# A 2x2 group of a filter's Toeplitz blocks by three products in place of four, with the shared product copied into the accumulators

## The chip, the core and the metric

The kernel runs on one core of a Trainium2 chip. The core has five engines, each with an instruction queue of its own: TensorE (matrix products, written to the accumulator memory PSUM), VectorE (elementwise work and reductions), ScalarE (functions of one input, copies), GpSimd (elementwise work, SBUF only in this kernel) and SyncE (it issues the DMA transfers here). In the profile they are PE, DVE, ACT, POOL and SP; PEld is TensorE's weight load. Operands lie in SBUF, 128 partitions wide. All numbers of the kernel are fp32.

The metric is the time of one launch on the device in microseconds, lower is better. Each version is run several times and the median is taken.

## The reference

The reference is one decoder layer on 16 sequences of 256 tokens and 512 channels, in three parts, each with a residual and a layer norm after it: a state-space part (two large projections, a short convolution, a scan), a long convolution along the channels, and a linear layer with eight low-rank experts of which each token takes two. The change is in the second part:

```python
vr = v.reshape(B, H, num_heads, L)       # v: the layer's x; x1 = x2 = ctx
kv = vr[:, :, :, None, :] * x2r[:, :, None, :, :]
y = irfft(rfft(kv, n=2 * L) * rfft(k, n=2 * L)[None, :, None, None, :])[..., :L]
y = y + kv * skip
out = jnp.einsum('bhijl,bhil->bhjl', y, x1r)
```

Here B = 16, L = 512, num_heads = 8 and H = 32. For each of the 32 filters ("heads" below) and each batch, 8 x 8 products `kv` of two signals of length 512 are convolved causally with the filter, multiplied with a third signal and summed over one of the two indices of 8.

## The kernel before

The causal convolution is done as a product with a lower triangular Toeplitz matrix of 512 x 512. It is cut into 4 x 4 blocks of 128: six full blocks below the diagonal and four triangular ones on it. A block depends only on the difference of its block numbers, so blocks (2, 1), (1, 0) and (3, 2) hold the same filter values, and so do (2, 0) and (3, 1). In each triangular block three of four 64 x 64 quadrants are not zero; these 12 quadrants are issued to TensorE's 64 x 64 tiles in three rounds of four (`QUADRANTS`), so that four run side by side. Halves of some blocks are swapped in the order of the channels (`SWAPPED_IN`, `SWAPPED_OUT`), so that each of the four tiles gets three quadrants. The second and the third round are kept apart from the first by a tiny copy on ScalarE, `one`: it waits for the first round, and the third round waits for it.

Stage one (the state-space part) goes over eight groups of 512 tokens and ends near 770 us. Stage two is the loop over `h`, the 32 heads, with software pipelining over neighbouring heads. A head has two halves of the batch, q = 0 and 1. For each half there is one call of `convolve` (six full products and the 12 quadrants, 512 columns wide) into four PSUM tiles of 128 x 512, held as two pairs: `y[0]` and `y[1]`. Each pair has one buffer only. The blocks of a pair in this version are (1, 0) and (3, 2), by `BLOCKS_OUT`; the full blocks come first and the quadrants after them, except where `late` is set (head 0 and the last convolution), where the order is the other way about.

Around a convolution the work is, by its line in the profile:

- VectorE: `products` (L152) makes `kv` of the next head from its turned input `vT` and the context `cT`, two operations for each q. `multiplied` (L963) reads a pair of `y` and makes `pr`; `reduced` (L973) sums it into `red`. L1085 adds this to `o`, which gives the convolution's output `ol`. `skip_sum` (L854) makes `ws`. `gates` (L1007 to L1027) ranks the eight experts by comparisons `cmp`, and ends with `xa`. `finish` (L1040) makes `x3` from the finished linear layer `base`.
- GpSimd: `skip_sums` (L844) makes `sk`; `skip_term` (L861) makes `t`; `with_residual` (L874, L876) makes `o` in three operations; the small steps of the layer norms (L986 to L994, L1045) make `nm`, `var`, `rs` and `nb`.
- ScalarE: copies `vT` (L142) and `xaT` (L1072) out of PSUM, `one` (L951), the sums and squares of the layer norms (L1065, L991), the exponential of the gates (L1011), and the result `res` (L1050).
- TensorE, beside the convolutions: the transposes of `vn` (L140), of `ol` (L1000) and of `xa` (L1070), the gates' logits `gl` (L1115), the linear layer `base` in four blocks (L1120), and its last term `lora` (L1076).
- SyncE: loads of the Toeplitz blocks `T` (L121), of `vn` (L133) and `cT` (L127), and the stores of `out` (L1051).

The order of the work on each engine is the order in which the code is written: the section is under `tc.manual_schedule()`, so nothing is moved by a planner. For head h the code issues: `multiplied` and `reduced` of q = 1 of head h-1; `ol`; `finish` of head h-2; the convolution q = 0; `products` q = 0 of the next head; `multiplied` and `reduced` of q = 0; the transposes and layer norm of `ol` (`centre`), with `skip_term` in between; `gl`; the four blocks of `base`; `gates`; the store; `products` q = 1 of the next head; `skip_sums`; the convolution q = 1, with the transpose of `xa` after its third full block; `lora`; and then the transposes and loads for the head after next. PSUM has eight tiles of 2 KB a partition: two in the pool `ps_t`, two in `ps_s`, four for `y`.

Of the kernel before, what the change touches and what calls it, by code (L numbers as in the profile page):

```python
# [14 lines left out]
P = 128  # L15
# [21 lines left out]
BLOCKS_IN, SWAPPED_IN = (0, 1, 2, 3), (1, 3)  # L37
BLOCKS_OUT, SWAPPED_OUT = (1, 0, 3, 2), (2, 3)

PAIRS = ((2, 0), (3, 0), (3, 1), (2, 1), (1, 0), (3, 2))  # L40
# [3 lines left out]
    (2, 0, 0), (0, 0, 1), (3, 1, 0), (1, 1, 1),  # L44
    (0, 0, 0), (2, 0, 1), (1, 1, 0), (3, 1, 1),
    (3, 0, 0), (1, 0, 1), (2, 1, 0), (0, 1, 1),
)
ER = NE * R
# [17 lines left out]
def decoder_kernel(  # L66
# [44 lines left out]
    ps_s = ctx.enter_context(tc.tile_pool(name="ps_s", bufs=2, space=PSUM))  # L111
# [4 lines left out]
    def load_T(h):  # L116

        both = big.tile([P, NQ * NL * BQ * NH * NH + 10 * P], F32, tag="big", name="kv")
        kv, T = both[:, 0 : NQ * NL * BQ * NH * NH], both[:, NQ * NL * BQ * NH * NH :]
        T = T.rearrange("p (k l) -> p k l", l=P)  # L120
        nc.sync.dma_start(T, toep[h])  # L121
        return kv.rearrange("p (q k b j i) -> p q (k b) j i", q=NQ, k=NL, j=NH, i=NH), T

    def load_c(h):

        cT = q3.tile([P, NQ, 6, BQ * NH], F32, tag="cT", name="cT")
        nc.sync.dma_start(cT, ctxT[h])  # L127
        return cT
# [36 lines left out]
    with ExitStack() as s1:  # L165
# [4 lines left out]
        gp = s1.enter_context(tc.tile_pool(name="gp", bufs=NI))  # L170
        ps_mm = s1.enter_context(tc.tile_pool(name="ps_mm", bufs=4, space=PSUM))
# [328 lines left out]
        for g in range(NG):  # L500
# [307 lines left out]
            if g == 0:  # L808
                skip_bc = wp.tile([P, S], F32, name="skip_bc")
                nc.sync.dma_start(skip_bc, skip.partition_broadcast(P))  # L810
                w_gl = wp.tile([P, KD, NE + ER], F32, name="w_gl")
                nc.sync.dma_start(w_gl, WglT.rearrange("(k p) e -> p k e", p=P))
                w_f = wp.tile([P, KD, D], F32, name="w_f")
                nc.sync.dma_start(w_f, WffnT.rearrange("(k p) o -> p k o", p=P))
                w_lb = wp.tile([ER, D], F32, name="w_lb")
                nc.sync.dma_start(w_lb, loraB)
                b_bc = wp.tile([P, D], F32, name="b_bc")
                nc.sync.dma_start(b_bc, b_ffn.partition_broadcast(P))
                gb_bc = wp.tile([P, NE], F32, name="gb_bc")
                nc.sync.dma_start(gb_bc, gate_b.partition_broadcast(P))  # L820

                tri = wp.tile([P, NE, NE], F32, name="tri")
                nc.gpsimd.memset(tri, 0.0)
                for e in range(1, NE):
                    nc.gpsimd.memset(tri[:, e, 0:e], 1.0)
                share = wp.tile([P, P], F32, name="share")
                nc.gpsimd.memset(share, 1.0 / D)
# [4 lines left out]
    with ExitStack() as s2:  # L832
        p2 = s2.enter_context(tc.tile_pool(name="r2", bufs=2, reuse_waits="tile"))
        ps_y = s2.enter_context(
# [36 lines left out]
        def with_residual(t, vT):  # L871

            o = p2.tile([P, NQ, NL, BQ * NH], F32, tag="o", name="o")
            nc.gpsimd.tensor_tensor(o[:, :, 1:3], t[:, :, 0::3], vT[:, :, 0::3], ALU.add)  # L874
            for a, b in ((0, HP), (HP, 0)):
                nc.gpsimd.tensor_tensor(  # L876
                    o[b : b + HP, :, 0::3],
                    t[a : a + HP, :, 1:3],
                    vT[a : a + HP, :, 1:3],
                    ALU.add,  # L880
                )
            return o
# [24 lines left out]

        def convolve(y, kv, T, q, between=None, pairs=PAIRS, late=False, early=None):

            begun = set()

            def full(lb, mb, stop):
                nc.tensor.matmul(  # L916
                    bank_of(y, lb),
                    T[:, PAIRS.index((lb, mb)), :],
                    moving(kv, q, mb),
                    start=not late and lb not in begun,  # L920
                    stop=stop,
                    skip_group_check=True,
                )
                begun.add(lb)

            def quadrant(lb, r, c):
                rows, cols = slice(r * HP, (r + 1) * HP), slice(c * HP, (c + 1) * HP)
                start = lb not in begun and (lb, c) not in begun
                begun.add((lb, c))
                return nc.tensor.matmul(  # L930
                    bank_of(y, lb)[cols],
                    T[rows, len(PAIRS) + lb, cols],
                    moving(kv, q, lb)[rows],
                    start=start,
                    stop=False,
                    skip_group_check=True,
                )

            def full_blocks():
                for n, (lb, mb) in enumerate(pairs):  # L940
                    if n == 1 and early is not None:
                        early()
                    if n == 3 and between is not None:
                        between()
                    full(lb, mb, n >= len(pairs) - 2)

            if not late:
                full_blocks()
            begin = [quadrant(*e) for e in QUADRANTS[:4]]
            one = p2.tile([P, 1], F32, tag="one", name="one")  # L950
            seen = nc.scalar.copy(one, nhalf[:, 0:1])  # L951
            for ins in begin:
                wait_for(seen, ins)
            for e in QUADRANTS[4:8]:
                quadrant(*e)
            for e in QUADRANTS[8:]:
                wait_for(quadrant(*e), seen)
            if late:
                full_blocks()

        def multiplied(y, cT, q, i):
# [4 lines left out]
                cT[:, q, 4 * i : 4 * i + 2].rearrange("p k (b i) -> p k b i", i=NH)  # L966
# [85 lines left out]

        vT_next, vns = heads["vT"], heads["vn"]
        sk_next = skip_sums(0, kvs[0][0])
        vT_after = turned_v(vns.pop(0))
# [12 lines left out]
        def turned_gates(xa):  # L1068
            xat = ps_s.tile([ER, P], F32, tag="s", name="xat")
# [8 lines left out]
        last, done = None, None  # L1078
        for h in range(HX):
            nxt, ff = h + 1 < HX, last is not None  # L1080
            if ff:
                o_f, red_f, y_f, cT_f = last
                contract(y_f, cT_f, red_f, 1, (0, 1) if h == 1 else (1, 0))
                o_l = p2.tile([P, NL, P], F32, tag="ol", name="ol")
                nc.vector.tensor_tensor(  # L1085
# [6 lines left out]
            (kv, T), cT, vT = kvs.pop(0), cTs.pop(0), vT_next  # L1092
            red = p2.tile([P, NQ, NL, BQ * NH], F32, tag="red", name="red")
            y = new_y()
            convolve(y, kv, T, 0, pairs=FIRST if h == 1 else PAIRS, late=h == 0)
            ws = skip_sum(sk_next)
            behind = None
            if nxt:
                kv_n, cT_n, vT_next = kvs[0][0], cTs[0], vT_after
# [3 lines left out]
            def skip():  # L1103
                skips.append(skip_term(cT, ws, behind))

            contract(y, cT, red, 0, (1, 0) if h else (0, 1))
            if ff:
                rs = centre(o_l, skip)
            else:
                skip()  # L1110
            o = with_residual(skips[0], vT)
            if ff:
                gl = ps_s.tile([P, NE + ER], F32, tag="s", name="gl")
# [4 lines left out]
                base = ps_s.tile([P, D], F32, tag="s", name="base")  # L1118
                for kc in range(KD):
                    nc.tensor.matmul(  # L1120
                        base, o_l[:, kc, :], w_f[:, kc, :], start=(kc == 0), stop=False
                    )
                xa = gates(gl, rs)
            if ready is not None:
                store(*ready)
            if nxt:
                products(vT_next, cT_n, kv_n, 1)
                sk_next = skip_sums(h + 1, kv_n)
            turned = []

            def turn():
                if ff:
                    turned.append(turned_gates(xa))

            y = new_y()
            if nxt:
                convolve(y, kv, T, 1, turn, FIRST if h == 0 else PAIRS, h == 0)
                if ff:
                    lora(base, turned)
            else:  # L1140
                y.append(ps_t.tile([P, BQ * NH * NH], F32, tag="tr", name="y2"))
                convolve(y, kv, T, 1, lambda: lora(base, turned), FIRST, True, turn)
            if ff:
                done = (h - 1, base, rs)
            if h + 2 < HX:
                vT_after = turned_v(vns.pop(0))
                kvs.append(load_T(h + 2))
                if h + 3 < HX:
                    vns.append(load_v(h + 3))
                    cTs.append(load_c(h + 3))  # L1150
# [5 lines left out]
        gl = ps_s.tile([P, NE + ER], F32, tag="s", name="gl")  # L1156
        base = ps_s.tile([P, D], F32, tag="s", name="base")
        o_l = {}

        def contracted(src, ks):  # L1160
# [4 lines left out]
            cs = 0 if ks[0] < 2 else 2  # L1165
# [42 lines left out]
        ready = finish(*done)  # L1208
        contracted(y_f[2].unsqueeze(1), (3,))
# [90 lines left out]
```

## Time and profile before

| | |
|---|---|
| median of three runs | 1501.47 us (1500.52 to 1502.03) |
| the profiled execution | 1501.61 us |
| its span, first to last instruction | 1499.8 us |
| granted TensorE clock in it | 0.998 |
| stage two, first quadrant to the end | 771.1 to 1499.8 us |
| from one head to the next | 22.46 us |
| DMA, share of the queues' time over the span | 0.20 |

A row of the profile's groups gives the line, the engine, the operation, the output and inputs by the program's names, the tile's shape and the count, then the busy time and the mean length of one; then the engine's idle time just before, and what ended it. A row of the timeline gives start and length in us, the engine and line, and a count where neighbours are merged. Idle time of an engine that is not the bottleneck costs nothing. Matmul rows overlap, because products are pipelined, so the spacing of their starts says more than their lengths.

### The profile page before, as it was taken

To read this page: it belongs to the slowest core of one execution; us is meant where nothing else is said; L and a number is where in the kernel's file an instruction comes from. 1 tells how busy PE (TensorE), PEld (TensorE's weight loads), DVE (VectorE), ACT (ScalarE), POOL (GpSimd) and SP (SyncE) were. 2 spreads that over 40 slices of the span, in tenths; PEclk is the share of its full clock that TensorE was granted. 3 is DMA by queue.
4 is the path that set the end of the run, shared out by engine and by line. 5 is a ranking of instruction groups with operands and counts; after the bars stand their busy time and mean duration, and the time that the engine had idled before them with its cause. 6 is when DMAs were issued, how large, how long until landed. Compare 5 with 4: busy or idle time off the path is not lost.

```text
span 1499.8 us, 18739 instructions
## 1 busy us (share of the span) xinstructions
PE 1480.3 (99%) x6952; PEld 936.5 (62%) x6952; DVE 1179.8 (79%) x2124; ACT 372.1 (25%) x843; POOL 367.9 (25%) x536
## 2 busy tenths in 40 slices
PE   9999999999999999999999999999999999999997
PEld 8777788887888878888754444444444444444443
DVE  5978778787787877878667778778778778778776
ACT  2522323233232322323101122122122122122121
POOL 7340010100101002010022243243243243243242
PEclk9999999999999999999999999999999999999999
DMA  8014021121111211112022212212212212212200
GB/s 284 31 36 133 18 69 43 36 79 36 52 43 36 79 43 49 38 37 86 8 95 70 85 49 78 85 50 78 85 49 78 84 50 78 84 50 78 84 33 21
DMA packets 50810, 97.46 MB, mean 65 GB/s; under 512 B 10656, under 2 KB 15008, under 8 KB 50720
## 3 DMA queue, kind: packets, MB, share of 16 engines
q1 hardware_dynamic: 50192, 96.28, 19.8%
q8 instruction: 54, 0.88, 0.2%
q14 instruction: 36, 0.29, 0.1%
q10 hardware_dynamic: 528, 0.00, 0.0%
HBM read 78.95 MB, written 17.32 MB: 64 GB/s over the span
## 4 chain that ended last, share of the span: by engine, by line
PE 92%; DVE 5%; DMA 1%; issue 1%; ACT 0%; POOL 0%; SPq 0%; POOLq 0%; DVEq 0%
PE y L916 22%; PE mm L302 17%; PE y L930 12%; PE s L302 11%; PE base L1120 7%; PE s L702 6%; PE mm L702 5%; PE base L1076 2%; PE gl L1115 2%; DVE acc L533 1%; PE tr L1000 1%; PE mm L788 1%; PE mm L661 1%; PE yps L604 1%; PE xm L543 1%; PE tr L140 1%
## 5 line engine op out<-in xcount | busy, mean ns | idle before, releaser
L916 PE MATMUL y<-kv 128*128 128x512 f32 x768 | 348.4, 597 | 0.3 <-DVE pr L963 0.3
L963 DVE TENSOR_TENSOR pr<-y,cT 128x1024 f32<-128x1024 f32 x126 | 148.5, 1219 | 129.6 <-PE y L930 126.0
L916 PEld LDWEIGHTS y<-kv 128*128 128x128 f32 x768 | 141.4, 191 | 158.9 <-issue 154.8
L930 PE MATMUL y<-kv 64*64 64x512 f32 x1536 | 179.6, 598 | 3.3 <-DVE xt L803 1.7
L152 DVE TENSOR_TENSOR kv<-vT,cT 128x1024 f32<-128x1024 f32 x128 | 150.4, 1217 | 1.4 <-ACT vT L142 1.4
L533 DVE SCALAR_TENSOR_TENSOR acc<-xi,wc,acc 128x512 f32<-128x512 f32 x192 | 145.9, 774 | 5.7
L973 DVE TENSOR_REDUCE red<-pr 128x128 f32<-128x1024 f32 x126 | 147.1, 1209 | 0.0
L930 PEld LDWEIGHTS y<-kv 64*64 64x64 f32 x1536 | 52.2, 132 | 122.3 <-issue 96.5
L1120 PE MATMUL base<-w_f,ol 128*128 128x512 f32 x248 | 111.5, 592 | 0.0
L302 PE MATMUL mm<-XT,w_z 128*128 128x256 f32 x384 | 90.7, 379 | 0.0
L302 PEld LDWEIGHTS mm<-XT,w_z 128*128 128x128 f32 x384 | 73.0, 190 | 9.9
L844 POOL TENSOR_TENSOR sk<-kv,skip_bc 128x512 f32<-128x512 f32 x32 | 47.3, 1480 | 115.1 <-DVE kv L152 115.1
L1120 PEld LDWEIGHTS base<-w_f,ol 128*128 128x128 f32 x248 | 44.8, 190 | 44.5 <-issue 44.5
L350 POOL TENSOR_TENSOR rstd<-ms,nhalf 128x4 f32<-128x4 f32 x8 | 8.1, 1018 | 257.9 <-DVE ms L348 257.9
L302 PE MATMUL mm<-xnT,w_z 128*128 128x256 f32 x288 | 70.0, 379 | 0.0
L986 POOL TENSOR_SCALAR nm_c<-sum_c 128x1 f32<-128x1 f32 x31 | 7.2, 231 | 249.4 <-DVE x L1040 249.4
L61 POOL TENSOR_TENSOR rs_a<-ve_a,nhalf 128x1 f32<-128x1 f32 x32 | 19.0, 594 | 189.0 <-DVE ve_a L59 180.5
L302 PEld LDWEIGHTS mm<-xnT,w_z 128*128 128x128 f32 x288 | 54.7, 190 | 10.9 <-issue 3.8
L302 PE MATMUL s<-XT,w_xi 128*128 128x256 f32 x256 | 60.5, 379 | 0.4 <-DVE XT L206 0.4
L302 PE MATMUL mm<-XT,w_xi 128*128 128x256 f32 x256 | 60.5, 379 | 0.0
L991 ACT ACTIVATE sq<-x,nm_c 128x512 f32<-128x512 f32 x31 | 22.4, 722 | 136.5 <-POOL nm_c L986 132.2
L302 PEld LDWEIGHTS s<-XT,w_xi 128*128 128x128 f32 x256 | 48.6, 190 | 7.3 <-POOL w_xi L216 0.8
(266 smaller groups left out, 2545.6 us busy)
## 6 DMA issues: line engine op xcount, KB each, us to landing
kv<-in_toep SPq DMA_DIRECT2D x32, 640.0 KB
cT<-in_ctxT SPq DMA_DIRECT2D x32, 384.0 KB
xt<-in_x SPq DMA_DIRECT2D x32, 256.0 KB
xnT<-in_xT SPq DMA_DIRECT2D x8, 1024.0 KB
spread<-both SPq DMA_DIRECT2D x32, 256.0 KB
first<-xt SPq DMA_DIRECT2D x32, 256.0 KB
vn<-first SPq DMA_DIRECT2D x32, 256.0 KB
out<-res SPq DMA_DIRECT2D x31, 256.0 KB
```

Source lines behind the costliest of these rows:

```text
L152: last = nc.vector.tensor_tensor(kv[:, q, k * BQ : (k + NL // 2) * BQ], vT[:, q, blks].rearrange("p k (b i) -> p (k b) i", i=NH).unsqueeze ...
L302: nc.tensor.matmul(ps, w[:, p, a, kc, :], Xs[b][:, kc, :], start=start and kc == 0, stop=stop and kc == 1, skip_group_check=upon,)
L533: nc.vector.scalar_tensor_tensor(acc, xi[:, :, k : k + S], wc[:, c, k : k + 1], acc, ALU.mult, ALU.add)
L702: nc.tensor.matmul(ps, own[a][c][:, n * P : (n + 1) * P], w_o[b][c], start=start and c == 0, stop=stop and c == HC - 1, skip_group_check=upon,
L844: nc.gpsimd.tensor_tensor(sk, own, skip_bc[:, h * NH : (h + 1) * NH].unsqueeze(1).to_broadcast(full), ALU.mult,)
L916: nc.tensor.matmul(bank_of(y, lb), T[:, PAIRS.index((lb, mb)), :], moving(kv, q, mb), start=not late and lb not in begun, stop=stop, skip_ ...
L930: return nc.tensor.matmul(bank_of(y, lb)[cols], T[rows, len(PAIRS) + lb, cols], moving(kv, q, lb)[rows], start=start, stop=False, skip_gro ...
L963: nc.vector.tensor_tensor(pr.rearrange("p (k b j) i -> p k b j i", k=2, j=NH), y[i].rearrange("p k (b j i) -> p k b j i", j=NH, i=NH), cT[ ...
L973: nc.vector.tensor_reduce(red[:, q, 2 * i : 2 * i + 2, :].rearrange("p k t -> p (k t)"), pr, AX.X, ALU.add)
L1076: nc.tensor.matmul(base, turned[0], w_lb, start=False, stop=True)
L1115: nc.tensor.matmul(gl, o_l[:, kc, :], w_gl[:, kc, :], start=(kc == 0), stop=(kc == KD - 1))
L1120: nc.tensor.matmul(base, o_l[:, kc, :], w_f[:, kc, :], start=(kc == 0), stop=False)
```

## The change

The 2 x 2 group of outputs 2 and 3 with inputs 0 and 1 has the blocks (2, 0), (2, 1), (3, 0) and (3, 1), of which (2, 0) and (3, 1) are equal. With T2 for these two, the outputs are T2 (x0 + x1) + (T1 - T2) x1 for block 2 and T2 (x0 + x1) + (T3 - T2) x0 for block 3. So three products stand for four:

- `prepared` gives the pair sum `xs` = x0 + x1 for each q and the two differences of blocks `Td`, on GpSimd, during the head before.
- `seeded` issues the shared product to a PSUM tile `yc`; ScalarE copies it into both tiles of `y[1]`, which now holds the blocks 3 and 2. The four remaining full products of a convolution and the quadrants add to `y` after that (`begun` starts with blocks 2 and 3, so no product of theirs starts afresh).
- Head 0's first convolution and the last convolution of all (`late`) keep six products.

The halves are swapped in another choice of blocks, so that equal blocks have equal layout. Of the diagonal, two triangles share one loaded block (`TRIANGLE_AT`); a quadrant of block 2 (`AGAIN`) is computed from a copy of the lower half of its input in the upper 64 partitions, `kvd`, made by two ScalarE copies a head (`again`). `T` has 7 blocks in place of 10, `cT` 7 parts in place of 6.

Around this: the pool `ps_s` lives in stage one only, and stage two gets `ps_b` with one tile for `yc` and one for `base`. `ol` is added on GpSimd, not VectorE. The last of the four blocks of `base`, the transpose of `xa` and `lora` move to the start of the next head, between its `multiplied` and `reduced`; so do the transposes of `vn` and the loads. `gates` comes after `products` of q = 1. The load of `lora_B` moves to the start of stage two. The last head keeps the earlier order of these.

```diff
+GIVEN = ((3, 2), (3, 0), (2, 0), (1, 0), (0, 0), (2, 2), (3, 3))
+FULL_AT = {(3, 2): 0, (2, 1): 0, (3, 0): 1, (2, 0): 2, (3, 1): 2, (1, 0): 3}
+TRIANGLE_AT = (4, 4, 5, 6)
...
 QUADRANTS = (
-    (2, 0, 0), (0, 0, 1), (3, 1, 0), (1, 1, 1),
-    (0, 0, 0), (2, 0, 1), (1, 1, 0), (3, 1, 1),
-    (3, 0, 0), (1, 0, 1), (2, 1, 0), (0, 1, 1),
+    (0, 0, 0), (3, 0, 1), (1, 1, 0), (2, 1, 1),
+    (2, 0, 0), (0, 0, 1), (3, 1, 0), (2, 0, 1),
+    (1, 0, 0), (1, 0, 1), (0, 1, 0), (3, 1, 1),
 )
+AGAIN = (2, 0, 1)
...
+            nc.gpsimd.tensor_tensor(o[:, :, 3], t[:, :, 0], vT[:, :, 0], ALU.add)
             for a, b in ((0, HP), (HP, 0)):
                 nc.gpsimd.tensor_tensor(
-                    o[b : b + HP, :, 0::3],
+                    o[b : b + HP, :, 0:3],
...
+        def prepared(kv, T):
+            xs = p2.tile([P, NQ, BQ * NH * NH], F32, tag="xs", name="xs")
+            Td = p2.tile([P, 2, P], F32, tag="Td", name="Td")
+            def pair_sum(q):
+                return nc.gpsimd.tensor_tensor(
+                    xs[:, q], moving(kv, q, 0), moving(kv, q, 1), ALU.add
+                )
+            def differences():
+                nc.gpsimd.tensor_tensor(
+                    Td, T[:, 0:2], T[:, 2:3].to_broadcast([P, 2, P]), ALU.subtract
+                )
+            return xs, Td, pair_sum, differences
+        def again(kv):
+            kvd = p2.tile([P, NQ, BQ * NH * NH], F32, tag="kvd", name="kvd")
+            for q in range(NQ):
+                nc.scalar.copy(kvd[HP:, q], moving(kv, q, 2)[0:HP])
+            return kvd
+        def seeded(y, T, xs, q):
+            yc = ps_b.tile([P, BQ * NH * NH], F32, tag="yc", name="yc")
+            nc.tensor.matmul(yc, T[:, 2, :], xs[:, q], start=True, stop=True)
+            nc.scalar.copy(y[1], yc.unsqueeze(1).to_broadcast([P, 2, BQ * NH * NH]))
...
+            begun = set() if late else {2, 3}
...
+                if (lb, r, c) == AGAIN:
+                    r, src, at = 1 - r, kvd[:, q], TRIANGLE_AT[3]
...
             if not late:
-                full_blocks()
+                full(1, 0, T[:, FULL_AT[1, 0], :])
+                full(3, 2, T[:, FULL_AT[3, 2], :])
+                full(3, 0, Td[:, 1, :])
+                full(2, 1, Td[:, 0, :])
...
+                order = (1, 0)
+                prs = [multiplied(y_f, cT_f, 1, i) for i in order]
+            y = new_y()
+            if h:
+                if rest is not None:
+                    base, o_r, xa = rest
+                    feed_forward(base, o_r, (3,))
+                    turned = turned_gates(xa)
+                seeded(y, T, xs, 0)
+                if rest is not None:
+                    lora(base, [turned])
+                if nxt:
+                    vT_after = turned_v(vns.pop(0))
+                    kvs.append(load_T(h + 1))
...
+            if ff:
+                for i, pr in zip(order, prs):
+                    reduced(pr, red_f, 1, i)
-                nc.vector.tensor_tensor(
+                nc.gpsimd.tensor_tensor(
                     o_l.rearrange("p k (q t) -> p k q t", q=NQ),
...
             contract(y, cT, red, 0, (1, 0) if h else (0, 1))
+            y = new_y()
+            def meanwhile():
+                skips.append(skip_term(cT, ws, behind))
+                if nxt:
+                    seeded(y, T, xs, 1)
             if ff:
-                rs = centre(o_l, skip)
+                rs = centre(o_l, meanwhile)
...
                 products(vT_next, cT_n, kv_n, 1)
+                more_next = prepared(kv_n, T_n)
+                more_next[2](0)
+                more_next[3]()
                 sk_next = skip_sums(h + 1, kv_n)
+                more_next[2](1)
+            if ff:
+                xa = gates(gl, rs)
             if nxt:
-                convolve(y, kv, T, 1, turn, FIRST if h == 0 else PAIRS, h == 0)
+                convolve(y, kv, T, Td, kvd, 1)
+                kvd_next = again(kv_n)
+                rest = (base, o_l, xa) if ff else None
```

## The prediction

> **What bounds the kernel now.** I read the busy totals first, then the costliest groups, then one head of the second stage in the timeline and in a table of windows, then the waits.
>
> The page's busy shares, and the table of windows for one head (columns: window, length, busy time of TensorE, its weight loads, VectorE, ScalarE, GpSimd, then granted clock, DMA share, GB/s):
>
> ```profile
> PE 1480.3 (99%) x6952; PEld 936.5 (62%) x6952; DVE 1179.8 (79%) x2124; ACT 372.1 (25%) x843; POOL 367.9 (25%) x536
> 1059.04:1081.50 22.46, 22.46 (x102) 9.65 (x100) 18.02 (x27) 4.52 (x12) 8.04 (x12) 1.00 0.22 71
> ```
>
> TensorE works through the whole 22.46 us of a head, VectorE 18.0, ScalarE 4.5, GpSimd 8.0. A busy TensorE row need not be a full one, so I look at how densely it is issued. The timeline of the head (start, length, engine, line, what, count):
>
> ```profile
> 1067.12 0.66 PE L1000 MATMUL tr<-ident,ol 128*128 128x128 f32 x4
> 1067.24 2.36 DVE L963 TENSOR_TENSOR pr<-y,cT 128x1024 f32<-128x1024 f32 x2 [0.54 <-PE y L930]
> ...
> 1067.61 1.09 PE L1115 MATMUL gl<-w_gl,ol 128*128 128x136 f32 x8
> ...
> 1068.54 3.60 PE L1120 MATMUL base<-w_f,ol 128*128 128x512 f32 x8
> ...
> 1071.98 2.74 PE L916 MATMUL y<-kv 128*128 128x512 f32 x6
> ```
>
> Eight base records take 1071.98 - 1068.54 = 3.44 us, 0.43 each. An fp32 product is two records, so a full 128x128x512 product costs 0.86 us. The next row starts where this one ends; nothing stands between. A head is 12 full products in two convolutions, two triangles of 2.74 us (12 quadrants of 64x64, four at a time), four base products, and small ones. The waits agree:
>
> ```profile
> DVE pr L963 <- PE y L930: 126.0, 61, 3.6
> ```
>
> VectorE waits for TensorE some 2 us before each pair of `pr`, while the whole page has only 0.3 us of TensorE idle ahead of full blocks and 3.3 ahead of quadrants. So TensorE's own work sets the 22.46 us.
>
> **What the skill says.** PSUM — Partial Sum Buffer, "The four PSUM rules": writes by ScalarE neither set nor clear the written bits; a matmul that doesn't start a group adds onto such data where an earlier matmul set the bit. The first head's convolutions set them, so the seed is added to; no run here shows a seed yet. The same page on bank collisions: different column tiles may write one bank at once, different row tiles may not. The trace shows the first half:
>
> ```profile
> 261.57 1.07 PE L543 MATMUL xm<-acc,mean 128*32 128x512 f32 x8
> ```
>
> Four column tiles into one bank, 3.44 us if serial, take 1.0. SBUF — State Buffer, "Who interferes with whom": a VectorE instruction with two SBUF inputs and a GpSimd one that reads SBUF block each other. The trace agrees: GpSimd's `rs_c` lasts 1.43 us beside the products of VectorE, and `cmp` on 64 elements 0.75 us until a GpSimd op is over:
>
> ```profile
> 1064.35 2.35 DVE L152 TENSOR_TENSOR kv<-vT,cT 128x1024 f32<-128x1024 f32 x2
> 1065.69 1.43 POOL L994 TENSOR_TENSOR rs_c<-var_c,nhalf 128x1 f32<-128x1 f32 x1
> ...
> 1071.61 1.52 POOL L876 TENSOR_TENSOR o<-t,vT 64x256 f32<-64x256 f32 x2
> 1072.47 0.75 DVE L1018 TENSOR_TENSOR cmp<-cmp,tri 128x64 f32<-128x64 f32 x1
> ```
>
> **The change, part by part.** *Products.* Each of 62 convolutions (all but the first and the last) goes from six full products to four, plus the shared one into `yc`: 62 x 0.86 = 53.3 us less of TensorE, 1.72 a head, hence 20.74. The quadrants stay twelve; the triangle is taken as 2.74.
>
> *Seed.* One ScalarE copy of 128x512 into 128x1024. `vT` (512 columns from PSUM) takes 0.59 us and `xaT` (128) 0.27, so 0.83 ns a column: 1.01 us for 1,024. Bounds: 0.59 (the read alone), and twice the estimate, 2.0, if PSUM to PSUM is slow.
>
> Put zero at the end of the second convolution of a head. TensorE does: last base block 0.86, `xat` 0.14, `yc` 0.86, `lora` 0.96, `vn` transposes 0.44, together 3.26. From there full blocks 3.44 + 0.18, triangle 2.74: end at 9.62. Then transposes 0.49, `yc` 0.86, `gl` 0.93, three base blocks 2.58: 14.48. Then 3.44 + 0.08 + 2.74: 20.74. This is the measured spacing of today's rows in the new order.
>
> Is each input there? `y0` must have been multiplied before the first full block: VectorE starts 0.12 after zero and needs 2.35 for two, done at 2.5, wanted at 3.26. The seed waits for `y1` (1.3) and `yc` (1.86), so about 2.0 to 3.0; the second full block wants it at 4.12. In the other half `y0` is done at 12.1, the seed at 12.0 (behind the statistics' first pass on ScalarE), wanted at 14.48 and 15.34. So the seed costs nothing under the moved base block, `lora`, `gl` and transposes; uncovered it would cost 1.3 + 1.0 + one `yc` 0.86 twice a head. A copy of 2.1 us would begin to show.
>
> *ScalarE* gets two seeds and two `kvd` copies (0.59 each from the same row): 4.5 + 3.2 = 7.7 of 20.74. Behind the seed wait the squares, hence `rs_b`, one us later; behind `kvd` only `xaT`. The `one` copies release the last four quadrants. In the first half `one` follows the square of `x3`, about 7.3, wanted near 8.6. In the second it now follows the exponential of the late gates, about 17.5 or a little more, wanted near 19.7. Both have room.
>
> *GpSimd* gets `ol` (1.08, from the 512-element row `t`), two pair sums (1.08 each) and the differences (256 elements, 0.73 as `o`); `o` is regrouped into 128, 384 and 384 elements, about 0.55 + 0.9 + 0.9 = 2.35 on the line through these two rows, in place of 2.2. 8.0 + 4.2 = 12.2 of 20.74. `ol` is ready near 6.0, wanted at 9.62. The pair sums come before 23 and are wanted from 21.7 and from 30.8; the differences are ready near 20, wanted near 26.
>
> *VectorE* loses `ol` (0.61). First half: 0.12 + 2.27 `pr` + 2.44 `red` + 0.67 `x3` + 0.60 `ws` + 2.35 products = 8.45, under 9.62. Second half, from 9.74: 2.27 + 2.26 + 2.35 + gates 2.56 = 19.2, under 20.86. It may come 2.35 us later before TensorE waits: `xat` wants the gates at 21.6, and `y0` must be done by 24.0.
>
> That margin is what GpSimd may eat. The products now come ahead of the gates and meet the `o` ops (two of about 0.9), and the gates meet pair sum, differences and `sk`. Each two-input VectorE op that meets a GpSimd op waits between nothing and the whole of it. In stage one six such ops took 6.78 us beside 256-element sums (1.13 each against an average 0.76 busy), so half an op is a fair wait:
>
> ```profile
> 60.48 6.78 DVE L533 SCALAR_TENSOR_TENSOR acc<-xi,wc,acc 128x512 f32<-128x512 f32 x6
> ```
>
> Half of two `o` ops, of one pair sum twice and of differences is 2.3; less the 0.53 that `cmp` waits already, I take 1.5 more. Lower end 0; upper end, whole ops: 0.9 + 0.9 + 1.08 + 0.55 + 1.48 = 4.9. At 1.5 nothing reaches TensorE.
>
> *DMA and rest.* Per head T falls 640 to 448 KB and `cT` rises 384 to 448. The loads of T, `vn` and `cT` move past `yc`, `lora` on TensorE, but their wait is the same convolution; T is first read by the differences, some 16 us later. The queue behind holds only `out`, whose `res` comes later. DMA share is 0.22; hidden. `lora_B` is loaded at the start of stage two, wanted two heads later. The first head has no covering work between its convolutions: about 0.2 lost.
>
> Sum: 1499.8 - 53.3 + 0.2 = 1446.7 for the span; this run took 1501.61, so 1.8 lies around it: 1448.5. The median of the runs is 0.1 lower. I say 1449.
>
> **Rivals.**
> 1. *GpSimd holds VectorE up.* For it: the waits above; six two-input ops against a train of GpSimd ops. Against: 2.35 us of room. An extra wait of 2.4 to 3.9 costs 0 to 1.5 a head, over 30 heads up to 45; middle 0.7, so 1449 + 21 = 1470. At the upper end of 4.9 it would be 2.55 a head, 1526; from 4.1 on the gain is gone.
> 2. *The seed copy is the wait.* A copy above 2.1 us, or ScalarE late for another reason, costs its excess once a head: 0.5 gives 1449 + 15 = 1464. Against: 1.1 us of room in the tighter half.
> 3. *Quadrants stop running four at a time* (the other side). Each of the second and third rounds now has two quadrants in one bank, before all four in different ones. In the second round they are also of different row tiles, which the skill warns of and no row shows. One serial pair is 0.86 on 64 convolutions, +55: 1504, no change. If both rounds pay, +110: 1559. It decides from 0.83 us a convolution on. Against: each pair writes different partitions, and `xm` shows column tiles sharing a bank at full rate.
>
> **How the numbers follow.** TensorE stays fed 0.64 (1445 to 1453); rival 1 short of the loss 0.17; rival 2 0.03; so faster 0.84. One serial pair or stalls that just eat the gain 0.04, within 0.2% (3 us, about what a measurement can tell). Slower 0.12: rival 3 in full 0.07, rival 1 beyond 4.1 0.05. The range 1444 to 1486 holds the likeliest case, rival 2 and nearly all of rival 1's gaining part, 0.81; the likeliest alone has 1445 to 1453.
>
> **What would show it.** Right: heads 20.7 us apart, TensorE's rows touching, triangles still 2.74, the seed near 1.0 us and `pr` of VectorE still waiting for quadrants. Rival 1: `xat` or the first full block waiting for VectorE, `cmp`, `ex` or products stretched. Rival 2: full blocks waiting for ScalarE. Rival 3: triangles of 3.6 us or more. Wrong at the root would be a full product not saved: L916's successor with other than 768 - 248 + 124 `y` and `yc` records.

## The result, and the profile after

| | before | after |
|---|---|---|
| median | 1501.03 us (1500.52 to 1502.03, 4 runs) | 1445.14 us (1444.09 to 1447.89, 4 runs) |
| ratio, 95% interval | | 0.963, 0.9613 to 0.9646 |
| profiled execution, its span | 1501.61, 1499.8 | 1447.89, 1446.1 |
| from one head to the next | 22.46 | 20.61 |

The change is faster by 55.9 us; 1449 was forecast, a gain of 52.5 from the 1501.47 known then. The busy totals of the changed kernel, and its table of windows over one head (columns as before):

```profile
PE 1425.9 (99%) x6828; PEld 915.6 (63%) x6828; DVE 1215.7 (84%) x2093; ACT 464.4 (32%) x969; POOL 567.8 (39%) x662
1039.82:1060.43 20.61, 20.61 (x97) 8.93 (x96) 19.11 (x26) 7.46 (x16) 14.41 (x16) 1.00 0.23 71
```

TensorE is as full as before over a head that is 1.85 us shorter. VectorE now has 19.11 of 20.61, before 18.02 of 22.46, although an addition left it. The profiled execution of after is the slowest of its four. Part of that lies ahead of the change: the first transposes of `vn` come at 766.85 us, before at 764.60. Another 1.3 us is one long head, shown below. From the first product of `kv` (768.11 and 765.85) to the end it is 678.0 against 734.0, 56.0 less, which is the difference of the medians to 0.1 us.

The timeline of the same head, after. First the start of the head, where the moved work and the seed stand:

```profile
1036.46 0.35 DVE L1074 SCALAR_TENSOR_TENSOR xa<-gl,den,ex 128x128 f32<-128x128 f32 x1
1036.59 1.12 PE L1133 MATMUL base<-w_f,ol 128*128 128x512 f32 x2
1036.76 2.35 DVE L1010 TENSOR_TENSOR pr<-y,cT 128x1024 f32<-128x1024 f32 x2
...
1037.56 0.27 PE L1123 MATMUL xat<-ident,xa 128*128 128x128 f32 x1
...
1037.67 1.02 PE L947 MATMUL yc<-xs,kv 128*128 128x512 f32 x2
...
1038.77 1.00 ACT L948 COPY y<-yc 128x1024 f32<-128x1024 f32 x1 [0.64 <-PE yc L947]
...
1039.82 1.88 PE L959 MATMUL y<-kv 128*128 128x512 f32 x4
...
1041.54 1.88 PE L959 MATMUL y<-kv,Td 128*128 128x512 f32 x4
...
1043.35 1.51 PE L977 MATMUL y<-kv 64*64 64x512 f32 x11
```

The convolution before ends at 1036.59. The seed lasts 1.00 us and is there at 1039.77, and the second full product, which adds to it, starts 0.86 after 1039.82. The four full products take 1039.82 to 1043.35, 3.53 us. The triangle goes from 1043.35 to 1046.09, 2.74. No product waits in this head. The same two rows before:

```profile
1059.04 5.42 PE L916 MATMUL y<-kv 128*128 128x512 f32 x12
...
1064.38 2.81 PE L930 MATMUL y<-kv 64*64 64x512 f32 x24
```

There the six full products took 1059.04 to 1064.38, 5.34 us, and the triangle, up to the next row at 1067.12, 2.74.

Then what GpSimd and VectorE do to each other, in the second half of the head before that:

```profile
1030.16 3.15 DVE L158 TENSOR_TENSOR kv<-vT,cT 128x1024 f32<-128x1024 f32 x2
1030.25 3.92 POOL L885 TENSOR_TENSOR o<-t,vT 64x384 f32<-64x384 f32 x2
...
1033.56 0.69 DVE L1063 TENSOR_TENSOR cmp<-lg 128x64 f32<-128x64 f32 x1
...
1034.24 1.27 POOL L924 TENSOR_TENSOR xs<-kv 128x512 f32<-128x512 f32 x1
1034.31 1.29 DVE L1065 TENSOR_TENSOR cmp<-cmp,tri 128x64 f32<-128x64 f32 x1
```

The two products take 3.15 us, before 2.35. The first `cmp` waits about 0.5 and the third 1.1 (the second, of the same shape, takes 0.21). As a result `xa` ends at 1036.81, 0.2 us after the convolution, and `pr` follows without a wait. TensorE wants `xa` at 1037.56: 0.75 us are left.

One head of this execution shows the edge. From the end of one head's second convolution to the next the others take 20.6 us (all but the first and the last), this one 21.9:

```profile
1221.66 1.48 POOL L853 TENSOR_TENSOR sk<-kv,skip_bc 128x512 f32<-128x512 f32 x1
1221.90 1.26 DVE L1069 SCALAR_TENSOR_TENSOR ex<-rank,ex 128x8 f32<-128x8 f32 x1 [0.48 <-ACT kvd L939]
...
1223.90 0.30 PE L1123 MATMUL xat<-ident,xa 128*128 128x128 f32 x1 [0.68 <-DVE xa L1074]
```

VectorE starts `ex` half a microsecond later than in other heads. Why is not to be seen. So `sk` has begun on GpSimd first, and `ex` takes 1.26 us in place of 0.19. Now the transpose waits 0.68 us for `xa`, and the first full product comes 0.94 later than in other heads. VectorE is late from there on, and the first triangle of the head takes 3.08 us in place of 2.74; two runs below, with one more operation and with `one` ahead, show by which chain.

### The profile page after: what moved, and what is told of

Same layout as the page of the kernel before. It is cut to its first block, busy times and chain, and to the rows that moved or that the text cites. A ratio compares the mean times of both kernels' runs of the same rounds, so it can differ in the third digit from the quotient of the medians.

```text
span 1446.1 us, 18895 instructions
## 1 busy us (share of the span) xinstructions
PE 1425.9 (99%) x6828; PEld 915.6 (63%) x6828; DVE 1215.7 (84%) x2093; ACT 464.4 (32%) x969; POOL 567.8 (39%) x662
## 4 chain that ended last, share of the span: by engine, by line
PE 90%; DVE 6%; issue 1%; DMA 1%; ACT 1%; POOL 0%; SPq 0%; POOLq 0%; DVEq 0%; ACTq 0%
PE mm L309 18%; PE y L959 15%; PE s L309 12%; PE y L977 12%; PE base L1133 8%; PE s L709 6%; PE mm L709 5%; PE yc L947 4%; PE gl L1198 2%; PE base L1129 2%; DVE acc L540 2%; PE tr L1047 1%; PE mm L795 1%; PE mm L668 1%; PE yps L611 1%
## 5 line engine op out<-in xcount | busy, mean ns | idle before, releaser
L158 DVE TENSOR_TENSOR kv<-vT,cT 128x1024 f32<-128x1024 f32 x128 | 180.0, 1447 | 1.4 <-ACT vT L148 1.4
L959 PE MATMUL y<-kv 128*128 128x512 f32 x272 | 128.1, 594 | 2.1 <-DVE pr L1010 1.2
L885 POOL TENSOR_TENSOR o<-t,vT 64x384 f32<-64x384 f32 x64 | 121.1, 1892 | 4.4
L959 PE MATMUL y<-kv,Td 128*128 128x512 f32 x248 | 116.5, 592 | 0.0
L959 PEld LDWEIGHTS y<-kv,Td 128*128 128x128 f32 x248 | 47.1, 190 | 59.3 <-issue 59.1
L959 PEld LDWEIGHTS y<-kv 128*128 128x128 f32 x272 | 49.0, 190 | 53.9 <-issue 50.6
L924 POOL TENSOR_TENSOR xs<-kv 128x512 f32<-128x512 f32 x63 | 80.4, 1276 | 2.4
L948 ACT COPY y<-yc 128x1024 f32<-128x1024 f32 x62 | 61.8, 997 | 34.0 <-PE yc L947 23.8
L1165 POOL TENSOR_TENSOR ol<-o,red 128x512 f32<-128x512 f32 x31 | 39.5, 1273 | 83.3 <-DVE red L1020 83.3
L977 PE MATMUL y<-kvd,kv 64*64 64x512 f32 x128 | 65.2, 589 | 0.0
```

What stands on the lines that cost most here:

```text
L158: last = nc.vector.tensor_tensor(kv[:, q, k * BQ : (k + NL // 2) * BQ], vT[:, q, blks].rearrange("p k (b i) -> p (k b) i", i=NH).unsqueeze ...
L885: nc.gpsimd.tensor_tensor(o[b : b + HP, :, 0:3], t[a : a + HP, :, 1:4], vT[a : a + HP, :, 1:4], ALU.add,)
L924: return nc.gpsimd.tensor_tensor(xs[:, q], moving(kv, q, 0), moving(kv, q, 1), ALU.add)
L948: nc.scalar.copy(y[1], yc.unsqueeze(1).to_broadcast([P, 2, BQ * NH * NH]))
L959: nc.tensor.matmul(bank_of(y, lb), w, moving(kv, q, mb), start=not late and lb not in begun, stop=False, skip_group_check=True,)
L977: return nc.tensor.matmul(bank_of(y, lb)[cols], T[rows, at, cols], src[rows], start=start, stop=False, skip_group_check=True,)
```

## The experiments

**Six products again.** In the changed kernel, convolutions get six full products and no seed; everything moved stays.

```diff
-            begun = set() if late else {2, 3}
+            begun = set()
-                full(1, 0, T[:, FULL_AT[1, 0], :])
-                full(3, 2, T[:, FULL_AT[3, 2], :])
-                full(3, 0, Td[:, 1, :])
-                full(2, 1, Td[:, 0, :])
+                for lb, mb in ((2, 0), (3, 0), (3, 1), (2, 1), (1, 0), (3, 2)):
+                    full(lb, mb, T[:, FULL_AT[lb, mb], :])
...
-                seeded(y, T, xs, 0)
...
-                    seeded(y, T, xs, 1)
```

> The changed kernel with the six full products of before in every convolution, no shared product and no seed; everything moved stays where the change put it, and the pair sums and differences are still computed, without use. Theory (the gain is TensorE's 62 saved products): 62 x 0.86 = 53.3 us come back, 1498 (1495 to 1502). Rival (the gain comes from the moved work, the addition on GpSimd or the new order): below 1475.

Measured: 1533.53 us, 2.2% slower than the kernel before (ratio 1.0216, 1.0201 to 1.0231). Both expectations fail. 88 us come back, 35 more than the products. Its timeline shows where the 35 are:

```profile
1060.98 3.56 DVE L158 TENSOR_TENSOR kv<-vT,cT 128x1024 f32<-128x1024 f32 x2
...
1066.36 1.56 DVE L1063 TENSOR_TENSOR cmp<-cmp,tri 128x64 f32<-128x64 f32 x1
...
1069.81 0.30 PE L1121 MATMUL xat<-ident,xa 128*128 128x128 f32 x1 [0.39 <-DVE xa L1072]
...
1070.47 1.13 PE L1127 MATMUL base<-w_lb,xaT 128*128 128x512 f32 x2 [0.36 <-ACT xaT L1123]
```

Without the seed on ScalarE the statistics of `ol` come earlier, so GpSimd's two long additions of `o` start 0.44 us ahead of the products, where in the changed kernel they start with them. The meetings fall out worse: products 3.56, the third `cmp` 1.56, and the transpose of `xa` waits. Then `lora` waits for the copy of `xa`. In the changed kernel the shared product covers this copy: it keeps TensorE at work while the copy is made.

**The same without the sums.** The pair sums and differences, unused in the run above, are left out, which takes three operations from GpSimd's work of a head.

> As the run with six full products, but the pair sums and differences, which nothing reads there, are left out too. In that run the gates ended late (five of their operations beside GpSimd) and the transpose of xa waited. Theory (62 products are worth 53 us, the other 35 were VectorE held up by GpSimd): the gates are in time again; without the shared product between xa's transpose and lora up to 0.3 us a head stays: 1498 to 1510. Rival (the moved work costs 35 us by itself whenever the six products are back): 1525 and above.

Measured: 1515.12 us. `xa` is in time, and 18 us are gone, but the time lies between the two expectations. The rest is the second wait, larger than I had put it:

```profile
1062.69 0.27 PE L1119 MATMUL xat<-ident,xa 128*128 128x128 f32 x1
...
1063.32 1.12 PE L1125 MATMUL base<-w_lb,xaT 128*128 128x512 f32 x2 [0.36 <-ACT xaT L1121]
```

From the transpose to `lora` are 0.63 us, of which the transpose is 0.11: 0.52 of waiting a head.

**And with a cover.** In addition, the transposes of `vn` go ahead of `lora`.

```diff
+                if nxt:
+                    vT_after = turned_v(vns.pop(0))
                 if rest is not None:
                     lora(base, [turned])
                 if nxt:
-                    vT_after = turned_v(vns.pop(0))
                     kvs.append(load_T(h + 1))
```

> As the run with six full products and without the sums, but lora comes after the transposes of vn, so that they cover the copy of xa. In that run lora waited 0.52 us a head for this copy. Theory (the saved products alone make the difference to the changed kernel): 31 x 0.44 = 14 us come back, 1515 - 14 = 1501, that is 1445 + 53 + at most 3. Rival (the moved work holds TensorE in another way): 1508 and above.

Measured: 1502.60 us (1501.82 to 1503.32, 12 runs), ratio to before 1.0008 (0.9999 to 1.0016): as long as the kernel before within 0.2%, and 1.6 us above the 1501 of the theory. Its head lasts 22.50 us:

```profile
1049.00:1071.50 22.50, 22.50 (x100) 9.77 (x99) 19.24 (x26) 5.66 (x14) 10.18 (x14) 1.00 0.19 65
```

So the moved work, in this order and without the sums, is neither gain nor loss. The whole gain, 55.9 us against before and 57.5 against this run, is the products and the small gaps that go with them. The first run was 30.9 us slower than this one: 18.4 went with the sums, whose work had made `xa` late, and 12.5 with the wait for the copy of `xa`. The other 4 of its 35 are the small gaps.

**The seed twice.**

```diff
-            nc.scalar.copy(y[1], yc.unsqueeze(1).to_broadcast([P, 2, BQ * NH * NH]))
+            for _ in range(2):
+                nc.scalar.copy(y[1], yc.unsqueeze(1).to_broadcast([P, 2, BQ * NH * NH]))
```

> The changed kernel with the seed copied twice, so 2.0 us in place of 1.0. Theory (the seed is hidden; in the tighter half it was there 0.9 us before the second full product wants it, in the other 3 us): at most 0.1 us a head, 1445 to 1449. Rival (the seed is what the convolution waits for): 1 us a head or two, 1475 or 1505.

Measured: 1454.82 us, 9.7 more than the changed kernel, 0.31 a head for 1.0 us more in each half. In the timeline:

```profile
1060.90 2.02 ACT L949 COPY y<-yc 128x1024 f32<-128x1024 f32 x2 [0.64 <-PE yc L947]
...
1061.95 2.15 PE L960 MATMUL y<-kv 128*128 128x512 f32 x4
...
1063.94 1.88 PE L960 MATMUL y<-kv,Td 128*128 128x512 f32 x4
```

The seed ends at 1062.92 and the second full product was due at 1062.81; with the way from ScalarE to TensorE it starts 0.27 late, and the four-record row is 2.15 long in place of 1.88. In the other half nothing waits. The time is above the 1445 to 1449 of the theory and far below the rival's 1475. So the single seed is hidden, but the room in the tighter half is about 0.7 us, not 0.9: the second product starts 0.16 us after the seed's end, and this way between the engines had been left out.

**One more operation on GpSimd.**

```diff
                 more_next[2](0)
+                more_next[2](0)
                 more_next[3]()
```

> The changed kernel with the first pair sum done twice on GpSimd, one more 128x512 operation of 1.27 us right beside the gates. Theory (VectorE has room left): ex waits about 0.7 us more, the gates end just before the transpose of xa wants them, 0 to 0.2 us a head, 1445 to 1451. Rival (what GpSimd takes from VectorE is already passed on to TensorE): 0.7 us or more a head, 1465 and above.

Measured: 1459.02 us, 13.9 more, 0.46 a head: more than the theory allowed, less than the rival. `xa` behaves as expected, and the transpose comes 0.06 us late; with it the first full product of the head comes 0.15 late. The larger part is elsewhere, in the first half:

```profile
1067.14 1.21 POOL L1033 TENSOR_SCALAR nm_c<-sum_c 128x1 f32<-128x1 f32 x1
...
1068.39 0.72 ACT L1038 ACTIVATE sq<-x,nm_c 128x512 f32<-128x512 f32 x1 [3.80 <-POOL nm_c L1033]
...
1069.11 0.18 ACT L993 COPY one<-nhalf 128x1 f32<-128x1 f32 x1
...
1069.34 1.09 PE L977 MATMUL y<-kv 64*64 64x512 f32 x8
```

`nm_c`, one element a partition, takes 1.21 us beside the products of VectorE. The square of `x3` waits for it, `one` stands behind the square in ScalarE's queue, and the third round of quadrants waits for `one`. The triangle takes 1067.27 to 1070.36, 3.09 us. In the changed kernel `nm_c` takes as long (1042.75 to 1043.96). What is new is that VectorE leaves the gates later, so that `x3` starts 1.94 us after the first full product in place of 1.46, and the chain behind it ends too late.

**The same with `one` ahead.** In the first half the convolution is issued between `nm_c` and the square, so that `one` comes first.

```diff
-            nm, rs = centred_squares(x3, total, "c")
+            nm, rs = centred_squares(x3, total, "c", between)
...
-            ready = finish(*done) if done is not None else None
-            convolve(y, kv, T, Td, kvd, 0, late=h == 0)
+            def first_half():
+                convolve(y, kv, T, Td, kvd, 0, late=h == 0)
+            ready = finish(*done, first_half) if done is not None else first_half()
```

> The run with one more pair sum on GpSimd, but in the first half the copy one is issued to ScalarE ahead of the square of x3. In that run the triangle of the first half took 3.09 us in place of 2.74, since one stood behind the square, the square behind nm, and nm behind the products. Theory (one is the tightest point): 0.35 us a head comes back, 1459 - 10 = 1449 (1446 to 1452). Rival (the late gates alone cost the 14 us): 1457 to 1460.

Measured: 1448.68 us, 10.3 less than with `one` behind. So the chain from `nm_c` to the quadrants is what cost 10.3 of the 13.9. The other 3.5 fit the head's start, where the first full product still comes 0.15 us late.

**`one` ahead, nothing else.**

> The changed kernel with one issued ahead of the square of x3 in the first half, nothing else. Theory (one comes just in time there, its third round of quadrants starts without a wait): no change, 1443 to 1447. Rival (it is late already): 1440 or less.

Measured: 1444.29 us (1443.75 to 1445.27): no change. In the changed kernel `one` ends at 1044.88 and the third round starts at 1045.12, where the second leaves off: just in time. This run has a long head too, of 21.6 us, but there the triangle stays at 2.74: the 0.3 us that it lacks to 21.9 are what `one` cost in that head.

**All of `base` in the first half.** No base product is kept for the start of a head.

```diff
-                    feed_forward(base, o_r, (3,))
...
-                feed_forward(base, o_l, (0, 1, 2) if nxt else (0, 1, 2, 3), True)
+                feed_forward(base, o_l, (0, 1, 2, 3), True)
```

> The changed kernel with all four base products in the first half, as before the change; none is left to cover the start of a head. Theory (cover to spare): the gates then end 0.65 us ahead of the convolution's end and the first full product waits about 0.1 us for y0, 1445 to 1450. Rival (the moved product is needed as cover): 0.86 us a head, 1470.

Measured: 1464.21 us, 19.1 more, 0.64 a head: between the two, nearer the rival. The head's start:

```profile
1062.95 2.36 DVE L1010 TENSOR_TENSOR pr<-y,cT 128x1024 f32<-128x1024 f32 x2 [0.80 <-PE y L977]
...
1064.67 0.60 PE L146 MATMUL tr<-ident,vn 128*128 128x128 f32 x4
...
1065.45 1.95 PE L959 MATMUL y<-kv 128*128 128x512 f32 x4 [0.18 <-DVE pr L1010]
...
1069.05 1.51 PE L977 MATMUL y<-kv 64*64 64x512 f32 x11
```

From the transposes to the first full product are 0.78 us in place of 0.44: it waits 0.34 for `y0`. And the triangle, 1069.05 to 1072.08, takes 3.03, 0.29 too long, by the same chain to `one`, since TensorE comes to it earlier. So the moved product gains its place twice: 0.34 us a head by covering `y0`, and 0.29 because TensorE reaches the quadrants later.

**`ol` on VectorE again.**

```diff
-                nc.gpsimd.tensor_tensor(
+                nc.vector.tensor_tensor(
                     o_l.rearrange("p k (q t) -> p k q t", q=NQ),
```

> The changed kernel with ol added on VectorE again, as before the change. VectorE waits 1.25 us in that half for the quadrants and ol takes 0.61. Theory (moving ol bought room, not time): 1444 to 1448. Rival (VectorE is the bound, so its work counts): 31 x 0.61 = 19, 1464.

Measured: 1444.40 us (1443.91 to 1445.14): no change. VectorE then waits 0.55 us before `pr` in that half in place of 1.25. What was moved to GpSimd here bought room in a place that had some. It also took room elsewhere: with `ol` on VectorE, `nm_c` is done in 0.23 us, before the products begin, and `one` waits 0.50 us for the quadrants instead of coming just in time.

**The gates ahead of the products.**

```diff
+            if ff:
+                xa = gates(gl, rs)
             if ready is not None:
                 store(*ready)
             if nxt:
                 products(vT_next, cT_n, kv_n, 1)
...
-            if ff:
-                xa = gates(gl, rs)
```

> The changed kernel with the gates ahead of the products of q = 1 again, as before the change. Then xa is ready early, and its late end can't hold the transpose, while VectorE's work and its meetings with GpSimd stay about as many. Theory (TensorE is fed in nearly every head; only a slip such as the one head of 21.9 us can be avoided): 1442 to 1448. Rival (the late gates cost time now): below 1440; or the products' lateness then holds the next head: above 1450.

Measured: 1443.51 us (1443.43 to 1443.86), ratio to before 0.9614 (0.9598 to 0.963). The interval overlaps that of the changed kernel, so it is not shown to be faster; it is as fast, with four runs close together. In its trace no head is long: from the first product of `kv` to the end it takes 676.7 us against 678.0, and the difference is the long head's 1.3.

## Why the prediction was right

*What bounds the kernel.* TensorE's own work, in both versions. With six products and no waits the time is that of before (1502.6); with the shared product it is 1445.1. Of the other parts, `ol` and the place of the gates leave the time as it is when they alone are put back. The last block of `base` does not: put back alone it costs 19.1 us, because the new order needs it at the head's start. The moved transposes, `lora` and the loads were not put back one by one.

*The products.* The counts are those forecast: 520 records of full products into `y` and 124 into `yc` in place of 768. 1.72 us a head were forecast and 1.85 came. The rest is gaps: six full products took 5.34 us, of which 5.16 are products; four take 3.53, of which 3.44 are. The transpose of `xa`, which cost 0.14 inside the convolution, is 0.11 outside. Over 30 heads this is the 3 to 4 us by which the forecast was too high; 1445.1 is at the lower edge of the 1445 to 1453 that I called likeliest.

*The seed.* 1.01 us by the columns, measured 1.00. It is hidden; the run with two seeds shows that at 2.0 it begins to cost. The Trainium skill's statement (PSUM — Partial Sum Buffer, "The four PSUM rules") that matmuls add onto ScalarE's data where earlier matmuls set the bits holds for 62 seeds a launch.

*GpSimd against VectorE.* I took 1.5 us of further waiting in the second half. By the rows it is 0.8 for the products, 0.4 for the first `cmp` and 0.5 more for the third than before: 1.7. Of the 2.35 us of room, 0.75 are left. My own terms, 2.3 less 0.53, give 1.8, and I had written 1.5. That the sum comes so near is partly luck, since its terms do not hold: `ex` and the differences add nothing in most heads, and the pair sums and `ol` take 1.27 us, not 1.08. I had read them from `t`, one of whose inputs is broadcast; the sums of stage one, with two full inputs (L205, 1.27), were the nearer row. The 64x384 adds of `o` take 0.99 us where VectorE does not meet them (in the covered run with six products), not 0.9. GpSimd is busy for 14.4 us a head, where 12.2 were forecast. One sign of being right came only by half: `pr` waits 1.25 us for the quadrants in the first half of a head, but none at the end of the second, where it follows `xa`.

*`one` in the first half.* This step failed. It cost nothing here but 0.34 us in the one long head. I put `one` at 7.3 us after the head's start, wanted near 8.6, with room. It comes at 8.1 to 8.3 and the round starts at 8.5, so that nothing is left after the weights are loaded. What I missed is `nm_c`: I let it run in 0.2 us, and it meets the products and takes 1.21:

```profile
1042.55 2.45 DVE L158 TENSOR_TENSOR kv<-vT,cT 128x1024 f32<-128x1024 f32 x2
1042.75 1.21 POOL L1033 TENSOR_SCALAR nm_c<-sum_c 128x1 f32<-128x1 f32 x1
```

I had seen that very thing in the rows of before for `rs_c`, and had not applied it to `nm_c`, which the moved addition pushes into the same place: with `ol` back on VectorE it takes 0.23.

*The rivals.* GpSimd as the brake: it happens in one head of the profiled execution, 1.3 us, and in every head when one more operation is added or the meetings shift. With 0.75 us of room left it was closer than my chance of 0.17 for its gaining part says. The seed as the wait: 0.27 a head only with a second copy. Quadrants in one bank: not so. A round is two passes, and a pass starts 0.43 us after the one before it. The second round, in which two quadrants of different row tiles write different partitions of one bank, starts its passes at 1044.28 and 1044.71, and the third starts at 1045.12, some 0.85 after the second began, as before (1065.29 and 1066.15):

```profile
1044.28 0.59 PE L977 MATMUL y<-kvd,kv 64*64 64x512 f32 x1
...
1044.71 0.59 PE L977 MATMUL y<-kvd,kv 64*64 64x512 f32 x1
...
1045.12 1.04 PE L977 MATMUL y<-kv 64*64 64x512 f32 x8
```

The warning that the prediction takes from the Trainium skill (PSUM — Partial Sum Buffer, "PSUM bank collisions raise a hardware error"), that different row tiles may not write one bank at once, did not apply to this pair, which ran side by side; its partitions differ, and the triangle takes 2.74 us.

## What to carry to other kernels

Fewer products for more sums paid here, where TensorE had no gaps, and the gain could be counted from the spacing of its rows; but the sums here go to engines that hold each other up, so count the meetings of two-input VectorE operations and GpSimd, the one-element ones too. Room is best measured by doubling one suspect: here a second seed, one more sum and one product less of cover each cost 10 to 19 us, though in the kernel itself TensorE waited for none of them in all heads but one. And when a part is undone for a test, look for what else it had been covering: six products in the new order were at first 31 us too slow, 18 from sums that nothing used and 13 from a copy that the shared product had covered.

## What the runs showed of the hardware

- The same GpSimd and VectorE work costs differently by its phase. In the changed kernel the two products take 3.15 us beside `o`; in the run with two seeds `o` comes about 2 us later, the products take 2.35 and the first `cmp` 0.22, and it is `rs_b` that stretches to 1.65 us, from 0.57. In the run with six products the products take 3.56.
- Between two back-to-back VectorE products a GpSimd operation gets in and makes the second wait: in the changed kernel the first takes 1.2 us and the second 2.0, beside two long additions of `o`. A GpSimd operation on one element a partition waits for the rest of a product (`nm_c`, 1.21 us; 0.23 before).
- Two quadrants of different row tiles, on different partitions of one PSUM bank, run side by side: the triangle with such a pair takes 2.74 us, as without it.
